# Layer 0's router: six batches' rows turned by VectorE blocks and a way through DRAM

## The chip, the core and the metric

The kernel runs on one core of a Trainium2 chip. The metric is the device time of one execution in microseconds, as the median of several runs. The engines are TensorE (PE; its weight loads are listed as PEld), VectorE (DVE), ScalarE (ACT), GpSimd (POOL) and SyncE (SP), which here issues most DMAs. Each engine works through its own list in order; engines wait for each other by semaphores.

## What is computed

Two transformer layers with the layer norm behind each block, on 8 batches of 512 tokens with 512 features, all in float32:

```
x = layernorm(x + attention0(x))     # causal, 16 heads of 32
x = layernorm(x + experts(x))        # 8 experts, the best 2 of each token
x = layernorm(x + attention1(x))     # 8 heads of 64, 2 groups of keys
x = layernorm(x + ffn(x))            # 1408 hidden units, integer weights
```

The change touches the router of the experts, which works on the rows x1 behind the first layer norm:

```
router_logits = x1 @ gate_weight.T + x1 @ (2 * lora_B @ lora_A).T      # 8 logits for each token
probs = softmax(router_logits);  weights, selected = top_k(probs, 2)
```

TensorE multiplies over the partitions, and the rows x1 come out of the layer norm with their tokens on the partitions. For the logits the features must lie there, so each batch's 512x512 rows are turned first.

## The kernel before

`attention0` runs over the batches b, in each over four groups g of four heads, and in each group over three units u of key tiles, (0), (1, 3) and (2). A unit is: scores `sc` of four heads on TensorE (L1264), exponentials `p` on ScalarE (L1268), the causal mask on GpSimd (L1273), and one unit later the products `av` with the values (L1288). The four heads' matrix products use 32 rows or 32 columns of the array each and run side by side. There is one buffer for `sc`, so the next unit's scores wait until the exponentials have read the last ones. VectorE adds up the units' `p` (L1296); sums over the keys (`rs`, L1303), a reciprocal and `aoT` end a group.

Between the units stands other work, put into slots (g, u) by `plan(b)`: queries and keys of the next group (`ps_q` L1200, `ps_k` L1208), values (`ps_v` L1193), and work of the batch before, pb = b - 1: its output projection (`ps_o` L1216) with the layer norm (L148 to L153, on VectorE, with two small operations on GpSimd), its turning and its routing. The router's part is

- `turn(pb, c)`: four 128x128 transposes on TensorE (L1228) into one bank of `ps_x1T`, and a copy into `x1T` by VectorE or ScalarE in turn (L162, L160); four calls, c = 0 to 3, in slots (2, 1) and (2, 2);
- `score(pb)` in slot (3, 0): four products `ps_logits` (L459), one for each c, and a copy to `logits` on ScalarE (L1238);
- `choose(pb)` in slot (3, 1): the selection, beginning with small products `ps_r` (L471).

All single products (`ps_q`, `ps_k`, `ps_v`, `ps_o`, `ps_x1T`, `ps_logits`, `ps_lora`, `rs`) share two PSUM banks, so each waits until the one before the last has been read out. `merge` (two LoRA products `ps_lora` L749, scaled by ScalarE L760 and added by GpSimd L762) also stands in slots (2, 0) and (3, 0). A scheduler orders the engines' lists in batches 0 to 6 by these slots and the dependencies; the last batch is written out by hand, and there the turning of batch 6 is in slot (2, 0). Batch 7 is turned behind the loop.

SyncE's list around this is: the normalised rows written to DRAM, four times 256 KB (`rows`, L156), the load of `xT` for the next batch (L1152), which waits until the key products have read its buffer, and the load of `x` (L1156) into the buffer that the turned rows leave. GpSimd adds a bias to the loaded `x` (L1382). `x1T` has one buffer, which `one_hot` uses too.

```
places = ((2, 0),) * 4 if last else ((2, 1), (2, 1), (2, 2), (2, 2))
for c, slot in enumerate(places):
    todo[slot].append(lambda c=c: turn(pb, c))
todo[(2, 1) if last else (3, 0)].append(lambda: score(pb))
todo[(2, 2) if last else (3, 1)].append(lambda: choose(pb))
```

Of the kernel before, what the change touches and what calls it, by code (L numbers as in the profile page):

```python
# [9 lines left out]
F32 = mybir.dt.float32  # L10
# [8 lines left out]
P = 128  # L19
NB = 8  # L20
S = 512
D = 512
NT = S // P
ND = D // P
# [39 lines left out]
class Inputs:  # L64
# [3 lines left out]
    def __init__(self, *aps):  # L68
        for name, ap in zip(self.names, aps, strict=True):
            setattr(self, name, ap)  # L70


class Env:
# [645 lines left out]
class Experts:  # L719
# [8 lines left out]
    def room(self, i):  # L728

        at = 4 * EXPERT + i * ND * 512  # L730
        return self.w[:, at : at + ND * 512].rearrange("p (u f) -> p u f", f=512)
# [270 lines left out]
class IntegerFfn:  # L1002
# [64 lines left out]
    def out(self, os, t, c, parts):  # L1067
        for i, h in enumerate(parts):
            self.nc.tensor.matmul(os[t], lhsT=h[:, ts(t, P)], rhs=self.weights(2 * NHID + c),  # L1069
                                  start=(c, i) == (0, 0), stop=(c, i) == (NHID - 1, 1))  # L1070
# [51 lines left out]
def attention0(env, guard, keep, routes, experts, dram, p_mm, tiles_ctx):  # L1122
# [4 lines left out]
    tc, nc, ins, xs, vec = env.tc, env.nc, env.ins, env.xs, env.vec  # L1127
# [3 lines left out]
    with ExitStack() as phase:  # L1131
        work = phase.enter_context(tc.tile_pool(name="a_work", bufs=1))
# [54 lines left out]
        def mm(shape, name):  # L1187
            return p_mm.tile(shape, F32, tag="mm", name=name)

        def value(b, t):  # L1190
            ps = mm([P, D], "ps_v")
            for c in range(ND):
                nc.tensor.matmul(ps, lhsT=xts[b][:, c, ts(t, P)], rhs=wv[:, c, :], start=c == 0, stop=c == ND - 1)  # L1193
            vs[t] = own.tile([P, D], F32, tag=f"v{t}", name=f"v{t}")
            nc.vector.tensor_tensor(vs[t], ps, row[:, 0, :], ALU.add)  # L1195

        def query(b, g):
            ps = mm([P, S], "ps_q")
            for c in range(ND):
                nc.tensor.matmul(ps, lhsT=wq[:, g, ts(c, P)], rhs=xts[b][:, c, :], start=c == 0, stop=c == ND - 1)  # L1200
            q = own.tile([P, S], F32, tag="q", name="q", bufs=2)
            nc.vector.tensor_scalar(q, ps, vec[:, V_BQ + g : V_BQ + g + 1], None, ALU.add)
            heads[b, g] = [q]

        def key(b, g):
            ps = mm([P, S], "ps_k")
            for c in range(ND):
                nc.tensor.matmul(ps, lhsT=wk[:, g, ts(c, P)], rhs=xts[b][:, c, :], start=c == 0, stop=c == ND - 1)  # L1208
            k = own.tile([P, S], F32, tag="k", name="k", bufs=2)
            nc.scalar.activation(k, ps, AF.Identity, bias=vec[:, V_BK + g : V_BK + g + 1])  # L1210
            heads[b, g].append(k)

        def project(b, t):
            ps = mm([P, D], "ps_o")
            for c in range(ND):
                nc.tensor.matmul(ps, lhsT=aoTs[b][:, c, ts(t, P)], rhs=wo[:, c, :], start=c == 0, stop=c == ND - 1)  # L1216
            nc.vector.tensor_tensor(xs[b][:, t, :], ps, xs[b][:, t, :], ALU.add)
            if t == NT - 1:
                env.layernorm(b, router.rows[S * b : S * (b + 1)])

        x1Ts, logits = {}, {}

        def turn(b, c):
            if c == 0:
                x1Ts[b] = work.tile([P, ND, S], F32, tag="x1T", name="x1T")
            ps = mm([P, S], "ps_x1T")
            for t in range(NT):
                nc.tensor.transpose(ps[:, ts(t, P)], xs[b][:, t, ts(c, P)], env.ident)  # L1228
            if b == NB - 2:
                nc.scalar.copy(x1Ts[b][:, c, :], ps)  # L1230
            else:
                env.evacuate(c, x1Ts[b][:, c, :], ps)

        def score(b):
            ps = mm([P, S], "ps_logits")
            router.logits(x1Ts.pop(b), ps)
            logits[b] = work.tile([P, S], F32, tag="logits", name="logits")
            nc.scalar.copy(logits[b], ps)  # L1238

        def choose(b):  # L1240
            router.choose(b, logits.pop(b), mm([P, NT, E], "ps_r"))

        def dispatch(b):
            router.dispatch(b, mm([P, NT, E], "ps_rank"))
# [3 lines left out]
        def one_hot(b, places):  # L1248
            if places[0] == 0:
                rooms[b] = work.tile([P, ND, S], F32, tag="x1T", name="one_hot")  # L1250
            return router.one_hot(b, rooms[b], places)

        def enter(rows):
            router.enter(mm([P, 2, E * E_TILES], "ps_table"), *rows)

        def scores(b, g, u):
            q, k = heads[b, g]
            sc = p_sc.tile([P, 4, S], F32, tag="sc", name="sc")
            width = 0
            for kt in UNITS[u]:  # L1260
                w = S - P * kt
                for j in range(4):
                    hs = slice(HD * j, HD * (j + 1))
                    nc.tensor.matmul(sc[:, j, width : width + w], lhsT=k[hs, ts(kt, P)], rhs=q[hs, P * kt :],  # L1264
                                     start=True, stop=True)
                width += w
            p = own.tile([P, 4, width], F32, tag=f"p{u}", name="p", bufs=2 if u == 0 else 1)
            nc.scalar.activation(p, sc[:, :, :width], AF.Exp, scale=scale)  # L1268

            at = 0  # L1270
            for kt in UNITS[u]:
                first = p[:, :, at : at + P]
                nc.gpsimd.affine_select(out=first, in_=first, pattern=[[0, 4], [1, P]], compare_op=ALU.is_ge, fill=0.0,  # L1273
                                        base=0, channel_multiplier=-1)
                at += S - P * kt
            return p
# [41 lines left out]
        def plan(b):  # L1318

            todo = {(g, u): [] for g in range(ND) for u in range(len(UNITS))}  # L1320
            for slot, places in (((0, 0), (0, 1)), ((0, 1), (3,)), ((0, 2), (2,))):
                todo[slot] += [lambda t=t: value(b, t) for t in places]
            for g in range(ND):
                nb, ng = (b, g + 1) if g + 1 < ND else (b + 1, 0)
                if nb < NB:
                    todo[g, 1].append(lambda nb=nb, ng=ng: query(nb, ng))
                    todo[g, 2].append(lambda nb=nb, ng=ng: key(nb, ng))
            pb, last = b - 1, b == NB - 1
            if b:
                places = ((1, 0), (1, 0), (1, 1), (1, 1) if last else (1, 2))  # L1330
                for t, slot in enumerate(places):
                    todo[slot].append(lambda t=t: project(pb, t))
                places = ((2, 0),) * 4 if last else ((2, 1), (2, 1), (2, 2), (2, 2))
                for c, slot in enumerate(places):
                    todo[slot].append(lambda c=c: turn(pb, c))
                todo[(2, 1) if last else (3, 0)].append(lambda: score(pb))
                todo[(2, 2) if last else (3, 1)].append(lambda: choose(pb))
                if not last:
                    todo[2, 0].append(merge)
                    todo[3, 0].append(merge)  # L1340
            if b == 0:
                todo[1, 0].append(lambda: router.merge_lora(mm([P, ND, E], "ps_wr")))
            if b > 1:
                todo[0, 2].append(lambda: dispatch(b - 2))
                todo[1, 1].append(lambda: enter(one_hot(b - 2, range(NT))))
            if last:
                todo[1, 2].append(soon)
                todo[2, 2].append(first_rows)
                todo[3, 1].append(lambda: dispatch(b - 1))
                todo[3, 2].append(begin)  # L1350
            return todo
# [23 lines left out]
        for b in range(NB):  # L1375
            todo = plan(b)
            for g in range(ND):
# [16 lines left out]
                for u in range(len(UNITS)):  # L1394
                    p = scores(b, g, u)
# [15 lines left out]
        b = NB - 1  # L1411
# [11 lines left out]
        for c in range(ND):  # L1423
            turn(b, c)
        tiles.step()
        score(b)
        merge()
        choose(b)
# [610 lines left out]
```

## Time and profile before

| | |
|---|---|
| median of 3 runs | 2284.05 us (2281.4 to 2284.93) |
| profiled execution | 2286.21 us, span 2284.5 us |
| PE busy | 2238.4 us, 98% of the span |
| DVE busy | 1242.0 us, 54% |
| ACT busy | 648.2 us, 28% |
| POOL busy | 496.2 us, 22% |
| mean DMA rate | 55 GB/s |
| granted TensorE clock, mean | 0.995 |

The span runs from the first to the last instruction of the profiled execution; the execution's own time is 1.7 us longer. Times inside a trace count from the span's start. In a row of the order of time the first number is the start and the second the length of a merged group; a number in brackets is idle time before it and what ended it. In a row of windows each engine's busy time is followed by its count of instructions; then come the granted clock, the busy share of the 16 DMA engines and the rate in GB/s. A landing time runs from the issue of a DMA to its completion.

### The profile page before, as it was taken

The numbers are of one execution on the slowest core, as the hardware profiler recorded it, in microseconds if no ns is written. First come the engines' busy times: TensorE is split into PE (matmuls) and PEld (weight loads), VectorE is DVE, ScalarE is ACT, GpSimd is POOL, SyncE is SP. The second block draws the span as 40 slices with busy tenths as digits, with TensorE's granted clock in tenths as the row PEclk, the third lists the DMA queues.
The fourth block names the chain that finished last, engine by engine and source line by source line (L and its number), as shares of the span: only waits on it lengthen the run. The fifth ranks groups of instructions, "written<-read, shape, count | busy, mean of one in ns | idle before, by whom it ended". The sixth has DMA issues, their size and how long they took to land. (4 is left out here: it accounts for less than half of the span.)

```text
span 2284.5 us, 24183 instructions
## 1 busy us (share of the span) xinstructions
PE 2238.4 (98%) x9430; PEld 1153.0 (50%) x9430; DVE 1242.0 (54%) x1976; ACT 648.2 (28%) x937; POOL 496.2 (22%) x489
## 2 busy tenths in 40 slices
PE   9999999999998999999999999999999999999997
PEld 3344444444443444444443334443343777887776
DVE  3457576566657433242216877787667544444443
ACT  2332322323323221111223323333332222222222
POOL 2232423313233241131115122322211000000000
PEclk9999999999999999999999999999999999999999
DMA  8010101101112224232224011100100100000000
GB/s 290 19 56 1 56 19 37 56 1 56 47 45 74 93 85 174 91 125 88 92 84 147 10 56 56 49 27 27 37 1 17 48 19 19 19 19 19 19 19 20
DMA packets 58444, 126.63 MB, mean 55 GB/s; under 512 B 6210, under 2 KB 6210, under 8 KB 58322
## 3 DMA queue, kind: packets, MB, share of 16 engines
q1 hardware_dynamic: 47040, 89.32, 11.1%
q0 software_dynamic: 10560, 34.61, 5.2%
q8 instruction: 77, 1.26, 0.2%
q10 hardware_dynamic: 722, 1.07, 0.1%
q14 instruction: 45, 0.37, 0.0%
HBM read 89.59 MB, written 35.39 MB: 55 GB/s over the span
## 5 line engine op out<-in xcount | busy, mean ns | idle before, releaser
L845 PE MATMUL ps_gu<-experts,xrT 128*128 128x512 f32 (+1 forms) x520 | 248.7, 601 | 0.0
L1268 ACT ACTIVATE p<-sc 128x2048 f32<-128x2048 f32 (+1 forms) x96 | 152.9, 1593 | 189.0 <-PE sc L1264 189.0
L1273 POOL TENSOR_SCALAR_AFFINE_SELECT p<-p 128x512 f32<-128x512 f32 x128 | 93.2, 743 | 380.1 <-ACT p L1268 374.0
L1060 DVE SCALAR_TENSOR_TENSOR hT<-ps_u,vec,sg 128x512 f32<-128x512 f32 x88 | 65.8, 748 | 198.4 <-PE ps_u L1055 198.4
L1069 PE MATMUL ps_f<-ffn_w,h_half 128*128 128x512 f32 x672 | 169.8, 393 | 1.6 <-DVE h_half L1064 1.1
L934 POOL TENSOR_TENSOR g_total<-g_total,r_inv 128x512 f32<-128x512 f32 x64 | 89.7, 1402 | 359.7 <-DVE r_inv L1617 283.3
L1617 DVE RECIPROCAL r_inv<-r_inv 128x512 f32<-128x512 f32 x32 | 106.9, 3339 | 97.5 <-ACT r_inv L931 97.5
L1587 ACT ACTIVATE p<-sc 128x1024 f32<-128x1024 f32 x128 | 124.0, 1021 | 125.9 <-PE sc L1584 125.9
L1296 DVE TENSOR_TENSOR p<-p 128x1536 f32<-128x1536 f32 (+2 forms) x96 | 129.2, 1345 | 38.7 <-POOL p L1273 21.7
L1069 PEld LDWEIGHTS ps_f<-ffn_w,h_half 128*128 128x128 f32 x672 | 124.3, 188 | 34.9 <-DVE h_half L1064 7.6
L1055 PE MATMUL ps_g<-x_high,ffn_w 128*128 128x512 f32 x352 | 141.0, 401 | 0.8 <-DVE x L1558 0.8
L848 DVE TENSOR_TENSOR h<-ps_gu,h 128x256 f32<-128x256 f32 x67 | 28.4, 423 | 205.6 <-ACT h L847 205.6
L1055 PE MATMUL ps_g<-x_low,ffn_w 128*128 128x512 f32 x352 | 139.0, 395 | 0.0
L1055 PE MATMUL ps_u<-x_low,ffn_w 128*128 128x512 f32 x352 | 138.8, 394 | 0.0
L1055 PE MATMUL ps_u<-x_high,ffn_w 128*128 128x512 f32 x352 | 138.6, 394 | 0.0
L862 PE MATMUL ps_y<-experts,hT 128*128 128x512 f32 (+1 forms) x272 | 127.9, 593 | 0.5 <-ACT hT L856 0.5
L1584 PE MATMUL sc<-qT,kT 64*128 64x512 f32 x512 | 127.2, 615 | 1.0 <-ACT qT L1505 0.7
L1200 PE MATMUL ps_q<-experts 128*128 128x512 f32 x256 | 121.2, 615 | 4.3 <-DMA experts<-in_xT 4.3
L845 PEld LDWEIGHTS ps_gu<-experts,xrT 128*128 128x128 f32 x520 | 89.6, 192 | 68.2 <-issue 68.1
L1606 PE MATMUL av<-p,v 128*64 128x512 f32 x512 | 123.7, 605 | 0.0
L1193 PE MATMUL ps_v<-experts 128*128 128x512 f32 x256 | 116.3, 602 | 2.1 <-DVE v L1195 2.1
L1552 PE MATMUL ps_o<-attn_out,aoT 128*128 128x512 f32 x256 | 117.3, 602 | 0.8 <-ACT r_inv L931 0.8
(256 smaller groups left out, 3532.3 us busy)
## 6 DMA issues: line engine op xcount, KB each, us to landing
results<-y SPq DMA_DIRECT2D x68, 256.0 KB, 2.0
x<-in_x SPq DMA_DIRECT2D x8, 1024.0 KB, 7.5
experts<-in_gate_up SPq DMA_DIRECT2D x8, 1024.0 KB, 11.7
rows<-x SPq DMA_DIRECT2D x32, 256.0 KB, 2.1
x<-rows SPq DMA_DIRECT2D x8, 1024.0 KB, 11.3
experts<-in_xT SPq DMA_DIRECT2D x7, 1024.0 KB, 5.5
out<-x SPq DMA_DIRECT2D x28, 256.0 KB, 2.3
ffn_i<-in_wq_ffn SPq DMA_DIRECT2D x11, 512.0 KB, 4.3
```

Of the source, the lines that this page charges most:

```text
L845: mm = nc.tensor.matmul(ps, lhsT=xT[:, c, :], rhs=self.weights(i, c), start=c == 0, stop=c == ND - 1)
L862: self.nc.tensor.matmul(ps, lhsT=hT[:, c, :], rhs=self.weights(i, ND + c), start=c == 0, stop=c == self.NI - 1)
L1055: nc.tensor.matmul(ps, lhsT=w[:, ts(dc, P)], rhs=x[:, dc, :], start=(dc, i) == (0, 0), stop=(dc, i) == (ND - 1, 1))
L1069: self.nc.tensor.matmul(os[t], lhsT=h[:, ts(t, P)], rhs=self.weights(2 * NHID + c), start=(c, i) == (0, 0), stop=(c, i) == (NHID - 1, 1))
L1193: nc.tensor.matmul(ps, lhsT=xts[b][:, c, ts(t, P)], rhs=wv[:, c, :], start=c == 0, stop=c == ND - 1)
L1200: nc.tensor.matmul(ps, lhsT=wq[:, g, ts(c, P)], rhs=xts[b][:, c, :], start=c == 0, stop=c == ND - 1)
L1268: nc.scalar.activation(p, sc[:, :, :width], AF.Exp, scale=scale)
L1296: nc.vector.tensor_tensor(total[:, :, P * kt :], total[:, :, P * kt :], p[:, :, at : at + w], ALU.add)
L1552: nc.tensor.matmul(ps, lhsT=state[b]["aoT"][:, c, ts(t, P)], rhs=w_out[:, c, :], start=c == 0, stop=c == ND - 1)
L1584: nc.tensor.matmul(sc[:, j, :], lhsT=st["kT"][hs, ts(kt, P)], rhs=st["qT"][g][hs, :], start=True, stop=True)
L1587: nc.scalar.activation(p, sc, AF.Exp, scale=scale)
L1606: nc.tensor.matmul(st["av"][HD * j : HD * (j + 1), :], lhsT=st["v"][:, kt, HD * j : HD * (j + 1)], rhs=p[:, j, :], start=kt == 0, stop=kt ...
```

## The change

For batches 0 to 5 (`by_blocks = NB - 2`) the four calls of `turn` are replaced by one call of `blocks` in slot (2, 0). VectorE transposes each of the four 128x512 row tiles in blocks of 32 by 32 within the partitions' groups of 32, four instructions a batch. Four DMAs then write the result to a DRAM tile, one for each group of 32 partitions, in pieces of 512 bytes, and one DMA reads it back into the same SBUF buffer with the features on the partitions, 8 KB for each. The tokens come back in another order (block, tile, lane and not tile, block, lane), so ScalarE's copy of the logits reads its bank in that order. Batches 6 and 7 are turned by TensorE as before; their calls stand in slot (2, 0).

In the lists of the changed kernel TensorE's sixteen transposes and the four copies are gone in six batches; VectorE's four block transposes stand behind the normalisation and ahead of the copy of `q`. SyncE's list is: `rows` four times, the four writes, the load of `x`, the read back, the load of `xT`. TensorE's logits stand behind the first of the next unit's scores, followed by both LoRA products. GpSimd's bias addition stands ahead of one mask, not behind it.

```
class Turn:
    N = P // 32
    def __init__(self, env, dram, n, name):
        self.nc, self.n = env.nc, n
        self.dram = dram.tile([P, ND, self.N, n * 32], F32, name=name)
    def blocks(self, room, t, x):
        out = room.rearrange("p (j t c) -> p j t c", t=self.n, c=32)[:, :, t, :]
        self.nc.vector.transpose(out, x.rearrange("p (j c) -> p j c", c=32))
    def out(self, room):
        for i in range(self.N):
            src = room[32 * i : 32 * (i + 1), :].rearrange("r (k j f) -> r k j f", j=self.N, f=self.n * 32)
            self.nc.sync.dma_start(out=self.dram.rearrange("(j r) k i f -> r k j i f", j=self.N)[:, :, :, i, :], in_=src)
    def back(self, room):
        self.nc.sync.dma_start(out=room, in_=self.dram.rearrange("p k i f -> p (k i f)"))
    def by_tile(self, a, turned):
        if turned:
            return a.rearrange("p (i t c) -> p t i c", i=self.N, c=32)
        return a.rearrange("p (t i c) -> p t i c", i=self.N, c=32)
...
+        by_blocks = NB - 2
+        turns = Turn(env, dram, NT, "turned0")
+        def room(b):
+            x1Ts[b] = work.tile([P, ND, S], F32, tag="x1T", name="x1T")
+        def blocks(b):
+            room(b)
+            flat = x1Ts[b].rearrange("p k s -> p (k s)")
+            for t in range(NT):
+                turns.blocks(flat, t, xs[b][:, t, :])
+            turns.out(flat)
+            turns.back(flat)
...
-            nc.scalar.copy(logits[b], ps)
+            if b < by_blocks:
+                nc.scalar.copy(turns.by_tile(logits[b], False), turns.by_tile(ps, True))
+            else:
+                nc.scalar.copy(logits[b], ps)
...
-                places = ((2, 0),) * 4 if last else ((2, 1), (2, 1), (2, 2), (2, 2))
-                for c, slot in enumerate(places):
-                    todo[slot].append(lambda c=c: turn(pb, c))
+                if pb < by_blocks:
+                    todo[2, 0].append(lambda: blocks(pb))
+                for c in range(0 if pb < by_blocks else ND):
+                    todo[2, 0].append(lambda c=c: turn(pb, c))
```

More of the change, by code (lines that the diff above doesn't have):

```diff
@@ L70, in __init__, with blocks, out, back @@
             setattr(self, name, ap)
+class Turn:
+    N = P // 32
+    def __init__(self, env, dram, n, name):
+        self.nc, self.n = env.nc, n
+        self.dram = dram.tile([P, ND, self.N, n * 32], F32, name=name)
+    def blocks(self, room, t, x):
+        out = room.rearrange("p (j t c) -> p j t c", t=self.n, c=32)[:, :, t, :]
+        self.nc.vector.transpose(out, x.rearrange("p (j c) -> p j c", c=32))
+    def out(self, room):
+        for i in range(self.N):
+            src = room[32 * i : 32 * (i + 1), :].rearrange("r (k j f) -> r k j f", j=self.N, f=self.n * 32)
+            self.nc.sync.dma_start(out=self.dram.rearrange("(j r) k i f -> r k j i f", j=self.N)[:, :, :, i, :], in_=src)
+    def back(self, room):
+        self.nc.sync.dma_start(out=room, in_=self.dram.rearrange("p k i f -> p (k i f)"))
+    def by_tile(self, a, turned):
+        if turned:
+            return a.rearrange("p (i t c) -> p t i c", i=self.N, c=32)
+        return a.rearrange("p (t i c) -> p t i c", i=self.N, c=32)
 class Env:
@@ L1221, in attention0 @@
         x1Ts, logits = {}, {}
+        by_blocks = NB - 2
[9 more added lines that the diff above has]
+            turns.back(flat)
         def turn(b, c):
             if c == 0:
-                x1Ts[b] = work.tile([P, ND, S], F32, tag="x1T", name="x1T")
+                room(b)
             ps = mm([P, S], "ps_x1T")
```

## The prediction

> **What bounds the kernel now.** I read the page first, then the engines' order of time around one transposition, then the waits of TensorE in the six batches concerned. The page gives the engine shares:
>
> ```profile
> PE 2238.4 (98%) x9430; PEld 1153.0 (50%) x9430; DVE 1242.0 (54%) x1976; ACT 648.2 (28%) x937; POOL 496.2 (22%) x489
> ```
>
> TensorE has almost no idle time, so work taken from it is time saved, and a wait given to it is time lost, one for one. VectorE is half free. TensorE's order of time in batch 3, where batch 2's rows are turned (columns: start, length, line, tile, count; a number in brackets is idle time and what ended it):
>
> ```profile
> 260.45 1.07 PE L1288 MATMUL av<-p,v 128*32 128x512 f32 x8
> 262.95 3.70 PE L1208 MATMUL ps_k<-experts 128*128 128x512 f32 x8
> 266.58 1.07 PE L1288 MATMUL av<-p,v 128*32 128x384 f32 x16
> 268.65 7.13 PE L1193 MATMUL ps_v<-experts 128*128 128x512 f32 x16
> ...
> 325.41 1.14 PE L1264 MATMUL sc<-q,k 32*128 32x512 f32 x8
> 328.55 1.15 PE L1264 MATMUL sc<-q,k 32*128 32x384 f32 x16 [0.58 <-ACT p L1268]
> 329.63 3.70 PE L1200 MATMUL ps_q<-experts 128*128 128x512 f32 x8
> 333.17 0.60 PE L1228 MATMUL ps_x1T<-ident,x 128*128 128x128 f32 x4
> 337.75 3.70 PE L1208 MATMUL ps_k<-experts 128*128 128x512 f32 x8
> 341.29 0.60 PE L1228 MATMUL ps_x1T<-ident,x 128*128 128x128 f32 x4
> 345.23 1.07 PE L459 MATMUL ps_logits<-x1T,r_wr 128*32 128x512 f32 x8
> 346.23 1.12 PE L749 MATMUL ps_lora<-lora 16*128 16x512 f32 x2
> 347.28 0.64 PE L1288 MATMUL av<-p,v 128*32 128x256 f32 x8
> 349.77 3.70 PE L1200 MATMUL ps_q<-experts 128*128 128x512 f32 x8
> ```
>
> The lines at 260 to 268 are the same stretch in the previous batch without transposes. From one batch to the next it repeats every 93.2 us.
>
> **What goes.** Up to `ps_k` the stretch takes 337.75 - 333.17 = 4.58 us with transposes and 262.95 - 260.45 = 2.50 without; from `ps_k` to the end of the scores 345.23 - 341.29 = 3.94 against 268.65 - 266.58 = 2.07. That is 2.08 + 1.87 = 3.95 us a batch, more than sixteen transposes of 0.13 us (2.24), because they also split the groups of four `av` products that otherwise run side by side. The copies (two of 0.68 on VectorE, two of 0.59 on ScalarE) lie on engines that wait anyway.
>
> **What the new order does with it.** TensorE's list in the changed kernel puts the logits behind the next `av` and the first of the four 128x384 scores. I lay it out from `ps_q` at 329.63: 3.54 to 333.17; 2.50 to `ps_k` at 335.67; 3.54 to 339.21; `av` 1.00 (266.58 to 267.58); scores of 512 at 340.21 to 341.28; `av` 0.57 to 341.85. The next scores share their bank with the exponentials, and rows 325.41 and 328.55 show 3.14 from one to the next: 343.35. So about 1.5 us of what is saved turns into a wait on ScalarE that logits and LoRA products used to fill. With 0.54 for the first score (347.85 to 348.39) the logits could start at 343.9. Behind them in TensorE's queue stand two LoRA products, the other scores and `ps_q`: 1.00 + 1.05 + 1.3 = 3.35 us to `ps_q`. If the turned rows were there, `ps_q` would start at 347.25 and not 349.77: 2.5 us a batch, 15 for six. Break-even is a start of the logits at 349.77 - 3.35 = 346.4.
>
> **When the turned rows are there.** The chain starts where VectorE ends the normalisation:
>
> ```profile
> 328.23 4.14 DVE L153 TENSOR_SCALAR x<-x,mv,rstd 128x512 f32<-128x512 f32 x4 [1.48 <-POOL rstd L151]
> ```
>
> The DMA issues (size of each, median us from issue to landing) and two windows (the last three columns: clock, DMA share, GB/s) price the way through DRAM:
>
> ```profile
> rows<-x SPq DMA_DIRECT2D x32, 256.0 KB, 2.1
> ...
> experts<-in_xT SPq DMA_DIRECT2D x7, 1024.0 KB, 5.5
> ```
>
> ```profile
> 1212.00:1213.00 1.00, 1.00 (x5) 0.34 (x6) 1.00 (x2) 0.59 (x1) 0.92 (x2) 1.00 1.06 209
> 1213.00:1214.00 1.00, 1.00 (x8) 0.17 (x4) 0.99 (x2) 0.00 (x0) 1.00 (x1) 1.00 1.04 236
> ```
>
> The normalisation ends at 332.37. Four block transposes are not in this trace; 128x512 f32 operations on VectorE take 0.55 (L153, median) to 1.03 (the same beside GpSimd, here). I take 0.69, as L148 and L1217, since nothing suggests the faster of these: 2.76, to 335.13. They stand ahead of the copy of `q`, which then ends near 335.9 and holds the bank of `ps_k` for 0.25 us; the wait for the logits swallows that.
>
> SyncE now holds four writes of 256 KB, the load of `x` (two batches on), the read back and only then `xT`. First bytes come 0.8 us after an issue (rows issued at 328.81 move from 329.6), so at 336.0. Each write reads 32 partitions in 512-byte pieces. The nearest row is the load of `attn_out` in 64 partitions: 207 to 238 GB/s at a full DMA share (the two windows), where full-width loads move 390. At 227 the 1.05 MB take 4.6 us, to 340.6, landing 0.6 later (2.1 - 0.8 - 0.7 of data), 341.2. The ends: 390 GB/s (2.7 us), and 512-byte packets that each last as long as the mean packet of this queue (11.1% x 16 x 2284.5 us / 47040 = 86 ns; 128 on each engine, 11.0 us).
>
> The load of `x` no longer waits for TensorE's transposes, so it is queued at about 337.0 behind the writes: 2.7 us of data, 340.6 to 343.3. The read back waits for the writes to land, is issued at 341.3 and moves behind `x`: 343.3 to 346.0, landing 0.7 later, at 346.7; a lone load of 1 MB (the `xT` row, 5.5 from its issue) gives 346.8. Logits start at 346.7, `ps_q` at 350.05: **+0.3 us a batch, +2 for six**. At 390 GB/s the rows are there at 344.8: -1.6 a batch, -10. At 86 ns a packet they are there at 353.1: +6.7, +40.
>
> The Trainium skill, "DMA: Bandwidth & Descriptors", section "Specifications", calls 512 bytes enough for line rate. By that the writes go at 390 GB/s and the sum is -10; the `attn_out` windows show that few partitions halve the rate whatever the piece, and I go by them.
>
> Two followers of the moved steps cost nothing. `xT`, now issued behind the read back, lands some 3 us after it, just before `ps_q` wants it. GpSimd's bias addition of 4.53 us (L1382) starts with the earlier `x` near 344.5 instead of 350.73, ahead of one mask (347.32 now, then 349), whose reader comes after `ps_q` near 354. ScalarE's strided copy of the logits (0.58) stands between the two LoRA products and is in the 1.05.
>
> **The clock.** From 341.85 to 346.7 TensorE would do one score of 0.54 us. The trace has one such gap, idle from 733.69 to 736.58 (PEclk is third from the right):
>
> ```profile
> 736.00:737.00 1.00, 0.42 (x2) 0.30 (x4) 1.00 (x6) 0.00 (x0) 0.00 (x0) 1.00 0.00 0
> 737.00:738.00 1.00, 1.00 (x4) 0.00 (x0) 1.00 (x6) 0.00 (x0) 0.00 (x0) 0.56 0.00 0
> 738.00:739.00 1.00, 0.27 (x3) 0.11 (x1) 0.85 (x5) 0.76 (x2) 0.08 (x1) 0.50 0.00 0
> ```
>
> The granted clock then stays at 0.50 to 743.96: 6.84 us, 3.4 lost. A wait of 1.76 us at 718.4 did nothing. The new gap is longer in all and broken once; I take a fall in four batches of six, at 1.7 to 3.4 us each: **+10** (bounds 0 and 20).
>
> The Trainium skill, "TensorE: Matmul & The Clock Gate", Part 1, halves the clock after a whole idle window of about 3.4 us. By it the two idle parts of 1.5 and 2.8 us need not trip it and the sum is +2; the trace halved after 2.9 us, so the row decides for +12.
>
> Sum: 2 + 10 = +12 us on the profiled execution's 2286.21; the median of the runs is 2.2 lower, so I predict 2296.
>
> **Rivals.** *Faster:* the writes run at full width's rate. It decides at the four writes, once their data take under 4.3 us (245 GB/s); at 390 it gives 2274, and the gap is then too short and too broken for the clock. For it: the four stores of the first `out` batch, also 1 MB from SBUF, move at 370 to 430 (1840.4 to 1843.0); against: they use all partitions and 2 KB pieces. *No change:* +2 with the clock kept, 2286. *Much slower:* packets at 86 ns, +40 and the clock in every batch, +15: 2339. For it: no row here shows 512-byte pieces; against: 86 ns is just 2 KB at 380 GB/s, so most of it is bytes. VectorE as the bound I leave out: it gains 2.76 - 1.36 = 1.4 us a batch and waited 8.7 us for `ps_q` at 353.5. That TensorE keeps the transposes is excluded by its list: only the last two batches have them.
>
> **How the numbers follow.** Forecast (+5 to +25) 0.55, faster 0.16, no change 0.14, much slower or between 0.15. The measurement tells 0.2% apart (4.6 us). Range 2275 to 2326: it takes in the fast writes nearly to their end and transposes of 1.03 us (+1.4 a batch, +8) on top of the clock's bound; half of the fast case and most of the slowest lie outside.
>
> **What would show it.** Right: four block transposes of about 0.69 on VectorE; the read back landing near 14.3 us after the normalisation; TensorE waiting near 2.8 us for a DMA before `ps_logits` and 1.5 before the score ahead of it, six times; windows at clock 0.50 behind some of these. Wrong: no DMA wait before the logits (then 2271 to 2275), or a wait above 7 us (then 2326 and more).

## The result and the profile after

The changed kernel takes 2332.48 us (median of 4 runs, 2332.18 to 2333.74) against 2282.77 for the kernel before on the same chip (2281.4 to 2284.93): 1.0218 times as long, 95% interval 1.0200 to 1.0236. The forecast was 2296 with a range up to 2326: the sign was right, the size was not. The profiled execution has a span of 2330.9 us and a mean granted clock of 0.976, where it was 0.995.

The page's engine shares:

```profile
PE 2252.2 (97%) x9334; PEld 1156.6 (50%) x9334; DVE 1251.2 (54%) x1988; ACT 642.4 (28%) x925; POOL 486.4 (21%) x489
```

TensorE has 96 instructions fewer and is busy 13.8 us longer: less work takes more time. Its waits between 90 and 830 us (us in total, times, longest):

```profile
PE ps_logits L491 <- DMA x1T<-turned: 30.0, 6, 5.2
PE sc L1313 <- ACT p L1317: 13.8, 13, 1.8
```

Six waits for the turned rows and six more on the exponentials (the kernel before has 7, 5.2 us in all), as the steps said; the forecast had 2.8 us for each of the first, and they are 5.0. TensorE's order of time in the third of these batches:

```profile
357.66 0.91 PE L1313 MATMUL sc<-q,k 32*128 32x384 f32 x2 [1.43 <-ACT p L1317]
363.50 1.93 PE L491 MATMUL ps_logits<-x1T,r_wr 128*32 128x512 f32 x8 [4.93 <-DMA x1T<-turned]
365.36 1.99 PE L781 MATMUL ps_lora<-lora 16*128 16x512 f32 x2
366.15 1.01 PE L1313 MATMUL sc<-q,k 32*128 32x384 f32 x2
366.38 1.06 PE L781 MATMUL ps_lora<-lora 16*128 16x512 f32 x1
...
369.84 6.16 PE L1232 MATMUL ps_q<-experts 128*128 128x512 f32 x8
```

The logits take 1.8 times as long as in the lines of before (1.07), `ps_q` 1.7 times (3.70). The logits start 19.74 us after the `ps_q` at 343.76, where the forecast had 17.07. The next `ps_q` starts 6.34 us after the logits and not 3.35. From batch to batch the stretch repeats every 101.0 us (logits at 161.89 and 666.94, five batches apart), where the same five batches took 93.3 each before (157.92 to 624.53): 7.7 us a batch, 46 in six. The two profiled executions lie 46.4 us apart (2286.21 and 2332.62); the rest of the 49.7 is that the median of the runs before is 3.4 below its profiled execution. Windows of 3.4 us over the same stretch (each engine's busy time; then clock, DMA share, GB/s):

```profile
357.80:361.20 3.40, 0.76 (x2) 0.15 (x2) 0.00 (x0) 0.00 (x0) 0.20 (x1) 1.00 1.03 349
361.20:364.60 3.40, 1.10 (x8) 0.20 (x8) 0.00 (x0) 0.00 (x0) 3.40 (x1) 0.50 0.97 373
364.60:368.00 3.40, 3.40 (x14) 1.49 (x11) 0.00 (x0) 1.06 (x2) 1.51 (x2) 0.50 0.11 41
...
374.80:378.20 3.40, 3.40 (x27) 1.66 (x25) 1.40 (x4) 0.23 (x1) 0.00 (x0) 1.00 0.00 0
```

The clock falls at 361.2, before the wait ends, and comes back only at 374.8: 13.6 us at 0.50, four windows of 3.41, though TensorE is listed as busy in three of them. It falls in all six batches, in one of them for five windows.

The way through DRAM on SyncE's queue:

```profile
348.93 3.79 SPq L93 DMA_DIRECT2D turned<-x1T  x4
352.88 1.24 SPq L1188 DMA_DIRECT2D x<-in_x  x1
356.32 0.33 SPq L96 DMA_DIRECT2D x1T<-turned  x1
```

VectorE's four block transposes take 2.48 us (forecast 2.76), from 346.43 to 348.91. From the first write's issue to the read back's, which waits until all four have landed, are 7.39 us (forecast 6.1), and from there to the logits 7.18 (forecast 5.4).

### The profile page after: what moved, and what is told of

It is laid out like the page before. It is cut to its first block, busy times and chain, and to the rows that moved or that the text cites. A ratio compares the mean times of both kernels' runs of the same rounds, so it can differ in the third digit from the quotient of the medians.

```text
span 2330.9 us, 24038 instructions
## 1 busy us (share of the span) xinstructions
PE 2252.2 (97%) x9334; PEld 1156.6 (50%) x9334; DVE 1251.2 (54%) x1988; ACT 642.4 (28%) x925; POOL 486.4 (21%) x489
## 3 DMA queue, kind: packets, MB, share of 16 engines
q10 hardware_dynamic: 722, 1.07, 0.1%
## 5 line engine op out<-in xcount | busy, mean ns | idle before, releaser
L1322 POOL TENSOR_SCALAR_AFFINE_SELECT p<-p 128x512 f32<-128x512 f32 x128 | 83.2, 663 | 415.2 <-ACT p L1317 408.6
L1232 PE MATMUL ps_q<-experts 128*128 128x512 f32 x256 | 134.2, 671 | 4.5 <-DMA experts<-in_xT 4.5
L1313 PE MATMUL sc<-q,k 32*128 32x128 f32 (+3 forms) x1024 | 117.8, 492 | 14.6 <-ACT p L1317 13.8
L1234 DVE TENSOR_SCALAR q<-ps_q,vec 128x512 f32<-128x512 f32 x32 | 23.7, 741 | 185.8 <-PE ps_q L1232 185.8
```

## Experiments

Two sizes were to be explained, the low clock and the late rows. The theory: most of the loss is the clock, which the work behind the wait does not bring back, the rest is the rows' lateness, and nothing else about the way through DRAM costs anything. Its main rival: the time is lost by the wait and the traffic themselves.

### Is it the wait or the clock behind it?

```
 def score(b):
+    if b < by_blocks:
+        warm(b, 8)      # 8 products wo x wo, 128x512, behind the first scores
     ps = mm([P, S], "ps_logits")
```

> The changed kernel with eight throwaway 128x512 products (weights wo against wo, into one of the shared banks, read by nobody) between the first scores of 512 and the logits in the six batches; they take 8 x 0.89 = 7.1 us at full clock, nearly the whole stretch in which TensorE stood between the scores at 354.5 and the logits at 363.5; the way through DRAM is unchanged. One theory (most of the loss is the clock that falls behind the wait): logits where they were, everything behind them at full clock, the next queries start 1.5 to 2 us earlier and end 2 to 2.5 us sooner again, 4 to 5.5 us a batch: 2300 to 2308, clock 0.99 or more. The rival (the loss is the waiting itself, the low clock only goes with it): 2325 to 2335.

2313.77 us: 18.7 less than the changed kernel, with a clock of 0.991, which lies between the two ranges. Part of the gain came, not all: the throwaway products ended 0.7 to 1.9 us before the rows, and in three batches the clock still fell. In one of them it fell at 359.85, at the end of a window in which TensorE was busy for 2.24 of 3.40 us, with logits and LoRA products. So I filled the rest:

```
-        warm(b, 8)
+        warm(b, 10)
```

> The run with eight throwaway products ended its wait 0.7 to 1.9 us before the rows came, and its clock still fell in three of six batches. With ten products (8.9 us) TensorE is busy until the rows are there. If the rest of that loss is the clock in those batches, it stays at 1.00 in all six and the time is 2300 to 2308, though TensorE does 10.7 us more of throwaway work than with eight; if it is the way itself, 2313 to 2322.

2307.70 us, as the first theory expected. TensorE does 10.3 us more of useless work than with eight products (6 x (8.85 - 7.13)) and the median is 6 us lower. Against the kernel before on each run's chip it is 4 us, and the two intervals overlap (1.0110 to 1.0150 and 1.0085 to 1.0140), so this step alone is not clear of noise; in the traces the batch repeats every 97.8 us in place of 98.9.

```profile
348.83 8.85 PE L1284 MATMUL ps_warm<-experts 128*128 128x512 f32 x20
357.61 1.06 PE L491 MATMUL ps_logits<-x1T,r_wr 128*32 128x512 f32 x8
```

There is no wait before the logits, and the clock is 1.00 in all six batches. Keeping the clock gave back 24.8 of 49.7 us, which is clear of noise (1.0218 against 1.0112); what is left is the stretch that TensorE must fill until the rows come.

### What the clock goes by

```
+for kind in (16 rows, 32 rows, 32 columns, 64 rows): 18 products of it, then 16 full ones
+for share in (0.36, 0.69, 0.53): 10 rounds of products and a VectorE operation between
+pauses of VectorE operations behind 13 full products, 3 times each length
+twice: a pause of 5.1 us, 6 products on 16 rows, 14 full ones
```

> Nothing of the layers is computed; out is a copy of x. TensorE runs stretches of eighteen 512-wide products without pause with 16 rows, 32 rows, 32 columns and 64 rows of the array, between stretches of full products; then full products with pauses at about 0.36, 0.53 and 0.69 of the time busy; then pauses of 1 to 6 us among full products; then a pause of 5 us with six products of 16 rows behind it. One theory (the clock goes by how much of the array works, summed over a window of 3.41 us): it falls to 0.50 under 16 and 32 rows and 32 columns though TensorE never idles, holds at 0.53 and 0.69 busy, falls at 0.36; behind the pause it stays low as long as the thin products run. The rival (only idle time counts): it holds at 1.00 through all products without pause, falls only behind pauses over about 3 us, and returns one window after any work starts.

Windows over the four kinds of products without pause (TensorE's busy time is the first column after the length): 16 rows in the first two lines, 32 rows in the next two, then 32 columns and 64 rows.

```profile
96.60:98.90 2.30, 2.30 (x7) 1.08 (x7) 0.00 (x0) 0.00 (x0) 1.00 0.00 0
99.20:125.10 25.90, 25.90 (x31) 9.66 (x29) 0.00 (x0) 0.00 (x0) 0.50 0.00 1
141.40:146.80 5.40, 5.40 (x14) 2.46 (x14) 0.00 (x0) 0.00 (x0) 1.00 0.00 0
147.00:167.00 20.00, 20.00 (x24) 7.22 (x22) 0.00 (x0) 0.00 (x0) 0.50 0.00 0
182.80:198.30 15.50, 15.50 (x37) 3.83 (x36) 0.00 (x0) 0.00 (x0) 1.00 0.00 1
212.30:227.90 15.60, 15.60 (x37) 6.61 (x37) 0.00 (x0) 0.00 (x0) 1.00 0.00 0
```

TensorE never idles in these lines, and the clock falls all the same under products on 16 and on 32 rows. It holds under 64 rows and, against the theory, under 32 columns: in these four, rows in use count and columns don't. One 256-wide full product every 1.22 us lost the clock, one 512-wide (0.87 us back to back) every 1.64 us kept it. Pauses of 2.33 us and less never lost it, 3.05 us did in two of three, 3.78 and more always; full products then brought it back in 3.4 or 6.8 us. With six products on 16 rows behind a pause of 5.1 us it stayed low for 17.1 us, from 703.2 to 720.2, all through the thin products (the first line) and 5.8 us beyond:

```profile
703.90:714.30 10.40, 10.40 (x12) 3.69 (x12) 0.00 (x0) 0.00 (x0) 0.50 0.01 2
714.40:719.80 5.40, 5.40 (x8) 2.30 (x8) 0.00 (x0) 0.00 (x0) 0.50 0.00 0
```

The rival is refuted. In the changed kernel the LoRA products, on 16 rows each, stand right behind the logits, so they can be moved:

```
-                    todo[3, 0].append(merge)
+                    todo[(1, 2) if pb < by_blocks else (3, 0)].append(merge)
```

> The changed kernel with the LoRA products that stand right behind the logits (slot (3, 0)) put into slot (1, 2), well ahead of the wait; the logits then stand behind the products av and ahead of all 384-wide scores. One theory (products on 16 rows don't bring the clock back, full ones do): behind the wait there are only logits, scores and queries, so the clock stays at 0.50 for two or three windows of 3.41 us in place of four: 1.7 to 3.4 us a batch less, 2312 to 2322. The rival (the low clock lasts as long as it does whatever the work): 2327 to 2335.

2302.04 us, 30.4 less, a bigger gain than either range allowed. Two windows behind the wait, and the waits:

```profile
355.20:358.50 3.30, 3.30 (x14) 1.22 (x14) 0.00 (x0) 0.59 (x1) 1.59 (x2) 0.55 0.08 29
358.70:362.00 3.30, 3.30 (x23) 1.74 (x15) 0.20 (x1) 1.88 (x1) 0.94 (x2) 1.00 0.00 0
```

```profile
PE ps_logits L491 <- DMA x1T<-turned: 25.0, 6, 5.4
PE sc L1313 <- ACT p L1317: 5.2, 7, 1.8
```

The clock is low for one window in four batches and for two in the others, in place of four or five. The edit also brings the wait for ScalarE back to 5.2 us in all (13.8 in the changed kernel), so of the 30.4 us at most 22 are the clock's, the LoRA products' own half clock among them. It also ends the splitting of the heads' scores, which in the changed kernel run one by one on 32 rows between the LoRA products (the row at 366.15); the two are not told apart. The wait for the rows is still 25.0 us in all, against 30.0: the way through DRAM is as late as before (in the third batch 14.6 us from the first write's issue to the logits, in both kernels), and well over half of its price is gone.

### Why the rows come late

```
-            nc.sync.dma_start(out=xs[b], in_=...)
+            with tc.issue_after(turns.last.ins):     # the read back
+                nc.sync.dma_start(out=xs[b], in_=...)
```

and the same for `xT`, whose load moves from group 2 to group 3; both from batch 2 on.

> The changed kernel with the loads of xT and x issued behind the read back, so that nothing else stands between the writes and the read back. The scheduler then puts the logits ahead of all 384-wide scores. One theory (the chain is late because the load of x takes bandwidth from the writes and stands ahead of the read back): writes landed about 355.2 and read back landed about 5 us later, near 360.4 instead of 363.4, so 3 us a batch less wait, minus 0.5 for the displaced score; the clock still falls: 2314 to 2322. The rival (the writes in 512-byte pieces and SyncE's issues set the chain, the load of x costs it nothing): 2328 to 2336.

2321.82 us, 10.7 less, about as expected, but for half the expected reason:

```profile
343.39 3.79 SPq L93 DMA_DIRECT2D turned<-x1T  x4
351.03 0.33 SPq L96 DMA_DIRECT2D x1T<-turned  x1
```

```profile
355.93 1.93 PE L491 MATMUL ps_logits<-x1T,r_wr 128*32 128x512 f32 x8 [5.25 <-DMA x1T<-turned]
```

The writes with nothing behind them take 7.64 us to the read back's issue, no less than before (7.39), and over the six batches 7.37 to 7.64 against 7.38 to 7.50: the load of `x` takes nothing from them. The logits follow at 355.93, 4.90 after the issue and not 7.18: standing ahead of the read back costs 2.3 us a batch. The wait is not shorter (33.3 us in all), since no score is left to do in it.

What the writes cost was measured alone, in six forms:

```
+few_small:  32 partitions, 512-byte pieces (the change)     +all_large: 128 partitions, 2 KB
+all_small: 128 partitions, 512-byte pieces                  +few_whole:  32 partitions, 8 KB rows
+few_large:  32 partitions, 2 KB pieces                      +two_queues: few_small from two queues
```

> Nothing of the layers is computed; out is a copy of x. 1.05 MB goes from SBUF to DRAM as four DMAs of 256 KB and is read back, twice in each of six forms: 32 partitions in pieces of 512 bytes (the change's form), all partitions in pieces of 512 bytes, 32 partitions in pieces of 2 KB, all partitions in pieces of 2 KB, 32 partitions in whole rows of 8 KB, and the change's form on two queues in turn. The theory of the prediction (few partitions cap the rate, whatever the piece): both forms of 32 partitions near 175 to 230 GB/s, all partitions in 512-byte pieces near 390. The rival (the pieces cap it): both forms of 512 bytes near 175, 32 partitions in 2 KB or 8 KB near 350 to 400. If SyncE's issues of 0.95 us cap it, the two queues reach over 230.

Windows inside the second turn's transfers, in the order of `few_small`, `all_small`, `few_large`, `all_large`, `few_whole`, `two_queues` (the last three columns: clock, DMA share, GB/s):

```profile
142.00:146.00 4.00, 0.00 (x0) 1.00 0.94 218
153.40:156.40 3.00, 0.00 (x0) 1.00 1.00 287
163.60:167.10 3.50, 0.00 (x0) 1.00 0.97 231
174.50:176.50 2.00, 0.00 (x0) 1.00 1.02 382
183.50:187.00 3.50, 0.00 (x0) 1.00 1.02 241
195.00:199.00 4.00, 0.00 (x0) 1.00 0.95 215
```

From the first issue to the read back's the six take 6.69, 5.42, 6.06, 4.10, 5.96 and 6.93 us. Few partitions alone add 2.0 us, small pieces alone 1.3, both 2.6: the prediction's theory holds for the rate (218 to 241 from 32 partitions, 227 taken), and the rival in part. The Trainium skill, "DMA: Bandwidth & Descriptors", section "Specifications", calls 512 bytes enough for line rate. Here all partitions in 512-byte pieces move 287 GB/s and in 2 KB pieces 382, and the measurement decides. The four issues take 3.51 us, but a second queue gains nothing, so they are not the limit. In the layer's kernels the writes take 7.4 to 7.7 us and not 6.69 (8.6 in the first batch of the two runs with throwaway products): in `clear` their data move at 176 GB/s from 344.5 to 350.5, with no load beside them. Why they are slower there is not settled. Writes over all partitions were not tried in the layer.

### Is the way through DRAM free where nobody waits for it?

```
-                todo[(2, 1) if last else (3, 0)].append(lambda: score(pb))
-                todo[(2, 2) if last else (3, 1)].append(lambda: choose(pb))
+                todo[(2, 1) if last else (3, 2)].append(lambda: score(pb))
+                if last: todo[2, 2].append(lambda: choose(pb))
+                if b > 1: todo[0, 0].append(lambda: choose(b - 2))
```

> The changed kernel with the logits in slot (3, 2), behind the next keys, and the selection in slot (0, 0) of the next batch (the last batch as before). One theory (the way through DRAM costs only where TensorE waits for it): the rows land at least 3 us before they are wanted, no wait for them, clock 0.99, the transposes and the split groups are gone: 15 to 24 us under the kernel before, 2258 to 2270. The rival (traffic, the moved queues and VectorE's list cost by themselves): 2280 or more.

> The kernel before, transposes on TensorE, with the logits and the selection in the same later slots. It tells whether a gain of the run with later slots comes from the slots. By both theories about no change: the logits only change places with other work on TensorE, 2276 to 2290.

The kernel before with these slots: 2282.95 us, no change (0.9996, 0.9986 to 1.0006). The changed kernel with them: 2291.36 us, 41 less than without, but still 1.0036 times the kernel before (1.0021 to 1.0050): a miss, in the rival's range. No wait for the rows is left; a new one is there, which the profile (of an execution of 2300.0 us) shows. First TensorE's waits (us in total, times, longest), then GpSimd's order of time:

```profile
PE av L1337 <- POOL p L1322: 25.7, 6, 5.2
```

```profile
351.14 4.50 POOL L1435 TENSOR_TENSOR x<-x,row 128x2048 f32<-128x2048 f32 x1 [5.56 <-DMA x<-in_x]
355.59 0.64 POOL L1322 TENSOR_SCALAR_AFFINE_SELECT p<-p 128x512 f32<-128x512 f32 x1
```

GpSimd waits for the load of `x`, adds a bias for 4.5 us, and only then masks the `p` that the next `av` needs; that starts at 356.28, after 4.39 us of waiting. The clock falls at this wait too, for 6.8 us in each of the six batches. The sum `x` is needed one batch later, so the addition leaves its old place (but for batch 0) and stands where GpSimd has 9 us to spare:

```
+                    if b and (g, u) == (0, 0):
+                        with tc.issue_after(last_mask[0].ins):
+                            add_bias(b)
```

> The kernel with later slots, and GpSimd's bias addition put behind the first mask of the next batch, where GpSimd is idle for 9 us, and no longer behind the load of x and ahead of the mask of the first unit of group 3. The run with later slots waited 4.4 us a batch for that mask (25.7 us in all) and had two windows of 3.41 us at half clock behind it. One theory (the way through DRAM is hidden there and the new wait is GpSimd's order alone): the wait goes, the clock stays, about 7 us a batch: 2248 to 2262, under the kernel before. The rival (another late thing stands right behind that mask, xT or the second masks): 2275 to 2291.

> The kernel before, transposes on TensorE, with the later slots and the same place for the bias addition. It tells how much of a gain belongs to GpSimd's order. Both theories: no wait on GpSimd to take away there, 2276 to 2288. If it gains as much as the changed kernel does, the gain is not that of the change.

The changed kernel with both edits takes 2255.21 us (2254.92 to 2255.46): 0.9862 times the kernel before (0.9846 to 0.9879), as expected and faster than both kernels. Its largest wait of TensorE left between 90 and 830 us is that of the scores for the exponentials, which the kernel before with both edits has too:

```profile
PE sc L1313 <- ACT p L1317: 8.7, 13, 1.8
```

The kernel before with both edits gains 0.4% too, 2276.17 us (0.9957, 0.9940 to 0.9973): with the slots alone it had waited 3.3 us for the same mask in one of its batches, and in its profiled execution that batch took 97.3 us in place of 92.3. The block transposes and the way through DRAM are therefore worth 2276.17 - 2255.21 = 21 us where they are covered: 88.53 us a batch against 92.31.

## Why the prediction was wrong, and where it was right

**What goes: right.** The forecast had 3.95 us a batch for the transposes and the split groups. With the wait gone, and the later slots in both kernels, the batch is 3.78 shorter. (The 2.24 us for sixteen transposes are 0.14 each, not 0.13.)

**The new order: right.** The wait on ScalarE before the second scores came six times, at 1.43 us where 1.5 was forecast.

**When the rows are there: too early by 2.7 us a batch.** Two terms failed. The writes' 6.1 us were 7.39: the rate of 227 was near what they do alone (218), but the layer's kernel does not reach that. And the read back's 5.4 us became 7.18. The sum had 2.0 of it for the load of `x` ahead and 3.4 for the read back itself, as if its data followed those of `x` at once; with nothing ahead of it, in `clear`, it takes 4.90 to the logits, and the load ahead costs 2.3 more. (`x` was also issued later, 3.95 us behind the first write and not 1.8, since the four writes' issues took 3.79; whether that cost anything was not tried.) With the forecast's +0.3 that is +3.0 a batch and 18 in all, where the sum had +2.

**The clock: the step that failed.** "I take a fall in four batches of six, at 1.7 to 3.4 us each: +10 (bounds 0 and 20)." It fell in all six. What is left of the 7.7 us a batch for it, 7.7 - 3.0 = 4.7 or 28 in all, is an estimate; the run with ten throwaway products puts it at 25. Both lie above the bound of 20. The bound itself was wrong. It came from the one gap in the trace, after which the clock was back in two windows, and I did not ask what had run in the second of them, from 740.6 to 744.0:

```profile
740.89 1.94 PE L1303 MATMUL rs<-p,ones 128*32 128x512 f32 x8
742.76 2.56 PE L845 MATMUL ps_gu<-experts,first_turned 128*128 128x512 f32 x4
```

Both use 128 rows. Behind the new wait stood LoRA products on 16 rows, and `clock_kinds` shows that such work holds the clock down. The Trainium skill, "TensorE: Matmul & The Clock Gate", Part 1, lets the clock rise after one busy window; here the window 364.60:368.00 is listed as busy throughout and the clock stays at 0.50, so what it counts is not the profile's busy time.

Together 18 + 28 = 46 of the 46.4 us between the profiled executions, by construction, since the 28 is what was left.

**The rivals.** *Faster* needed writes at over 245 GB/s: they reach 218 alone. *No change* needed the clock kept, and the rows when forecast. *Much slower* came near the size, 2339, for the wrong reason: it put 40 us on slow packets and 15 on the clock.

**The range and the sign.** The terms named for the upper end add up to 2314 (2284 + 2 + 20 + 8), so 2326 stood on more than was named. The sign of being wrong tied 2326 and more to a wait above 7 us; the time came with waits of 5.0, because the clock behind them cost more than its bound.

**"Two followers of the moved steps cost nothing": right only under cover.** In the changed kernel GpSimd's early bias addition lay behind the longer wait for the rows. Once that wait was gone it cost 25.7 us of waiting by itself. The sentence named the mask and its reader, but not the price should the cover go. `xT` cost nothing, as forecast: TensorE never waited for it between 90 and 830 us.

## What to carry to other kernels

Price a new wait of TensorE by the work that stands behind it, not only by its length: products on 16 rows did not bring the clock back here, and moving them away was worth more (30.4 us) than getting the rows 2.3 us earlier (10.7). The way round through DRAM paid here only once its reader stood a whole landing later, and the chain to lay out then holds every issue of the queue and everything moved ahead of the read. When a wait is taken away, look on each other engine for what waits for a load of the same queue, and what stands behind it: here GpSimd's mask was late next.

## What was not expected of the hardware

- Products on 16 or 32 rows lose the clock without a single idle moment (after 2.4 and 5.5 us), products of 32 columns over all rows keep it for 15.5 us, products on 64 rows for 15.6.
- Useless full products made the kernel faster: ten in each of six batches, 53 us of TensorE's time in all, against 24.8 us less in the total.
- Writes in 512-byte pieces from all partitions move 287 GB/s against 382 in 2 KB pieces; from 32 partitions the size of the pieces matters little (218, 231, 241).
- One issue of a 256 KB write in 512-byte pieces holds SyncE's queue for 0.88 to 0.95 us from 32 partitions and for 0.66 from all; in 2 KB pieces from all partitions it is 0.45.
